# Turning the input of the query product on VectorE instead of TensorE, and moving one softmax scan, in a four-layer graph network kernel

## The chip, the cores and the metric

The kernel runs on one core of a Trainium2 chip. A core has five engines that run side by side and wait for each other through semaphores: TensorE (PE in the profile; its weight loads are listed as PEld), VectorE (DVE), ScalarE (ACT), GpSimd (POOL) and SyncE (SP, which here only issues transfers). Sixteen DMA engines move data between the device memory and the on-chip memory SBUF. TensorE writes its results into PSUM[...]. The metric is the device time of one execution, in microseconds. Before the change it was 3124.89 us, the median of three runs from 3123.66 to 3126.61.

## The reference

The input x has 128 graphs of 128 nodes with 256 features each, in float32. Four layers follow each other, and each is `x = layernorm(x + layer(x))`. The change touches the beginning of layer 0 alone, a graph attention:

```python
Xq = (H @ W_lin.T).reshape(bt, n, h, dh)
Xv = (H @ W_val.T).reshape(bt, n, h, dh)
e = jnp.einsum('behd,hd->beh', jax.nn.leaky_relu(Xq[:, src] + Xq[:, dst], 0.2), a)
e = e + jnp.log(A0[src, dst] + EPS)[None, :, None]
m = jax.ops.segment_max(e.transpose(1, 0, 2), src, num_segments=n)
ex = jnp.exp(e_t - m[src])
attn = ex / jax.ops.segment_sum(ex, src, num_segments=n)[src]
Y = jax.ops.segment_sum(attn[..., None] * Vt, src, num_segments=n)
...
return Y @ W_out.T
```

Here H is x, and there are 512 edges, 4 heads of 64 features. Layer 1 mixes over the graph and multiplies by weights three times (256 to 512 to 1024 to 256 features, ReLU between), layer 2 multiplies by three weight matrices and mixes with parts of the adjacency, and layer 3 is a two-layer network with two batch norms over all nodes, so it needs a pass over all graphs before its second half.

## The kernel before

**Tiling.** The graphs are worked on in 32 quads of four. A quad's x in the layout nodes x (graph, feature) is one tile of 128 partitions and 1024 floats, 512 KB. A product with weights contracts over features, so features have to lie on the partitions: the input must be transposed first.

**Staging.** `start` and `iteration_0` fill the pipeline; then `iteration(k)` runs for k = 1 to 32, and in each pass five quads are in work at different stages: layer 3 of quad a = k-1, layer 1 of c = k, the attention output of b = k+1, the softmax of e = k+2, and the queries and values of g = k+3. Quads 4 to 31 pass through this as g, in 28 passes. All instructions are recorded in the order in which the code writes them (a manual schedule): each engine executes its own in that order, and waits on semaphores where one needs another engine's result. Pools of tiles with a fixed number of buffers hand out SBUF and PSUM; a tile that takes a used buffer waits for its last reader.

**Products in seven parts.** Most products are split into 2x2 blocks and done in seven block products instead of eight (class `Seven`, and by hand in `second`), with sums of blocks ahead (S1 to S4 by `sums_a`, T1 to T4 by `sums_b`, on VectorE) and totals behind.

**The stretch around the change.** `second(c, between)` is the largest product of layer 1: fourteen steps of four matmuls each (L580), with copies on ScalarE (`keep`, L586), totals on VectorE (`total`, L592) and ReLUs on ScalarE (`relu`, L596). After step i it calls `after(i)`, which runs what the caller put into `between[i]`; this is how work of other quads is laid between the block products. In the passes concerned, `between[11]` holds the first step of the softmax of e (a transpose of its scores on TensorE, L385, and four copies by ScalarE, L387), then `values_in(g, quads[g].xg)`, then `query_sums(g)`. `values_in` (L236) transposes the quad's x: eight 128x128 transposes on TensorE (L245) into two PSUM tiles, which VectorE copies to SBUF as `xt` (L247). `query_sums` (L318) then makes S1 to S4 out of blocks of `xt` (L181 to L184, tile `xs`). `between[12]` holds the next two softmax steps, the two scans of the running maximum (L389, L391). Behind step 13 comes the last total of `second`.

**What follows in a pass.** The load of the next quad's x, `load_x(g + 1, "xg", 1, xpool)` (L205), into the only buffer of its tag; the remaining softmax steps (L394 and on); `stage_f` (L801), whose result `ag` ScalarE copies out (L804); then the queries of g (`queries`, L289, with L306 for its kept parts) and `hidden` (L837, with sums L188 to L191) in turns. The queries are written to device memory (`spill`, L268) by a DMA that SyncE issues, and gathered from there by GpSimd along the edges (L336); VectorE works on the gathered rows (`score`, L368 to L371). SyncE issues its transfers in order: the store of x3 (L788), the load of xg, the spill, the store of z (L858), the load of the attention weights (L427), the load of xr.

**Blocks of a product.** `node_blocks(tiles, room)` takes two tiles that hold two graphs each, in which `tiles[j][:, :, c, :]` is half c of the features of graph pair j. It is called by `query_sums` and by `first_seven`.

Of the kernel before, what the change touches and what calls it, by code (L numbers as in the profile page):

```python
# [8 lines left out]
F32 = mybir.dt.float32  # L9
# [17 lines left out]
def gnn_stack(ctx: ExitStack, tc: tile.TileContext, x, adj, w_qv_t, a, w_out_t, src, dst,  # L27
# [14 lines left out]
    nc = tc.nc  # L42
    B, N, D = x.shape
    H, DH = a.shape
    E = src.shape[0]
    P = 128
    assert N == P and D == 2 * P and E == 4 * P and H * DH == D and DH == 64
    NE = E // P
    DC = D // P
    QB = 4  # L50
# [34 lines left out]
    xpool = ctx.enter_context(tc.tile_pool(name="xpool", bufs=1))  # L85
# [43 lines left out]
    with ExitStack() as phase:  # L129
# [63 lines left out]
        quads = [Quad() for _ in range(NQ)]  # L193

        def cload(shape, name, ap, eng=None, dtype=F32, pool=cst):
            t = ctile(shape, name, dtype, pool)
            (eng or nc.sync).dma_start(t, ap)
            return t
# [4 lines left out]
        def load_x(q, tag="xr", bufs=3, pool=wk):  # L203
            t = pool.tile([P, QB, D], F32, tag=tag, name=f"{tag}{q}", bufs=bufs)
            nc.sync.dma_start(t, x[q * QB:(q + 1) * QB].rearrange("b n d -> n b d"))  # L205
            return t

        quads[0].xr = load_x(0)
        wqv = cload([P, DC, 2 * D], "wqv", w_qv_t.rearrange("(c p) f -> p c f", p=P), pool=xpool)
        a_sb = cload([P, N], "adj", adj)  # L210
# [22 lines left out]
        def temp(name):  # L233
            return wk.tile([P, 512], F32, tag="t", name=name, bufs=6)
# [42 lines left out]

        def node_blocks(tiles, room):

            a = {f"A{j + 1}{c + 1}": tiles[j][:, :, c, :] for j in range(2) for c in range(2)}  # L280
            for i in range(4):
                a[f"S{i + 1}"] = room[i // 2][:, (i % 2) * 256:(i % 2 + 1) * 256].rearrange("p (b n) -> p b n", b=2)
            sums_a(a, a)
            return a
# [13 lines left out]
        def queries(k, kept_at):  # L298
# [16 lines left out]

            return Seven(node_product(blocks, queries.blocks), part, out)

        def query_sums(k):  # L318
            quads[k].x_blocks = node_blocks(quads[k].xts, [temp("xs") for _ in range(2)])

        def gather(k):

# [179 lines left out]
        def first_seven(k):  # L502

            s = quads[k]
            room = room_of("adc", 4)
            a = node_blocks([s.mx[0], s.mx[2]], room)

            def part(bank, i):

                to = room[2 + i % 2]  # L510
                nc.scalar.copy(to, bank)
                return to

            def out(row, col, bank, kept_):
                h1 = temp("h1")
                if kept_ is not None:
                    nc.vector.tensor_add(h1, bank, kept_)
                nc.scalar.activation(h1, bank if kept_ is None else h1, AF.Relu)
                for t in range(2):
                    for c in range(2):  # L520
                        s.h1[2 * row + t, 2 * col + c] = h1[:, (2 * t + c) * P:(2 * t + c + 1) * P]

            return Seven(node_product(a, first_seven.blocks), part, out)
# [377 lines left out]
        def iteration(k):  # L901
            a, c, b, e, g = k - 1, k, k + 1, k + 2, k + 3
            has_c, has_b, has_e, has_g = c < NQ, b < NQ, e < NQ, g < NQ
            if has_b and b > 2:
                quads[b].xr = load_x(b)
            if has_c:
                late_sums(c)
            parts = quads[a].layer2
            if not has_c:

                h = quads[a - 1].hidden
                h.p6()
                for _ in range(4):
                    next(parts)
                next(parts)
                h.p7()
                for _ in parts:
                    pass

                def amid():  # L920
                    run(h.p4, h.p3)
                    hidden_stats(a - 1)

                stage_f(a, amid)
                for i in range(K3):
                    hidden_last(a, i)
                return
            steps = softmax_parts(e) if has_e else iter(())
            if has_c:
                between = {i: [] for i in range(14)}  # L930
                for i in (0, 1, 2, 3, 5, 7):
                    between[i].append(lambda: next(parts, None))
                between[11].append(lambda: next(steps, None))
                if has_g:
                    between[11] += [lambda: values_in(g, quads[g].xg), lambda: query_sums(g)]
                between[12] += [lambda: next(steps, None)] * 2
                if has_e:
                    for c_, i in enumerate((0, 2, 4)):
                        between[i].append(lambda c_=c_: score(e, c_ + 1))
                if has_b:  # L940
                    for j, i in enumerate((5, 8, 9, 10)):
                        between[i].append(lambda j=j: by_row(b, j))
                second(c, between)
            if has_g and g + 1 < NQ:
                quads[g + 1].xg = load_x(g + 1, "xg", 1, xpool)
            elif has_g:
                kept["w2t"] = xpool.tile([P, K3, D], F32, tag="xg", name="l3w2", bufs=1)
                nc.sync.dma_start(kept["w2t"], l3_w2_t.rearrange("(c p) f -> p c f", p=P))
            if has_c:
                room = room_of("m2", 7)  # L950
            next(steps, None)
            if has_g:
                q = queries(g, room[:3])
            stage_f(a)
            if not has_b:
                last_sums()
                h = quads[a].hidden = hidden(a, room[5:] + room[3:5])
                for _ in third(c, 0):
                    pass
                rest = third(c, 2)  # L960
                next(rest)
                third_mix(c, 0)
                third_norm(c, 0)
                for _ in rest:
                    pass
                h.p1()
                third_mix(c, 2)
                third_norm(c, 2)
                lower = kept["m2"][:, :3 * 512].rearrange("p (t f) -> p t f", t=2)
                quads[c].layer2 = layer2(c, None, lower)  # L970
                next(quads[c].layer2)
                run(h.p5, h.p2)
                next(quads[c].layer2)
                return
            h = hidden(a, room[5:] + room[2:4])
            if has_g:
                q.p1()
            next(steps, None)
            if has_g:
                run(q.p5, q.p2, q.p6)  # L980
            run(h.p1, h.p5)
            next(steps, None)
            if has_g:
                q.p7()
            run(h.p2, h.p6)
            next(steps, None)
            if has_g:
                run(q.p4, q.p3)
                spill(g)
            h.p7()  # L990
            if has_b:
                aggregate(b)
            run(h.p4, h.p3)
            hidden_stats(a)
            if has_g:
                gather(g)
            if has_b:
                stage_a(b)
            for _ in third(c, 0):
                pass  # L1000
            if has_e:
                attention(e)
                scatter(e)
            rest = third(c, 2)
            mix1(b, 0)
            mix1(b, 2)
            third_mix(c, 0)
            next(rest)
            w = first_seven(b)
            third_norm(c, 0)  # L1010
            next(rest)
            run(w.p1, w.p5, w.p2)
            next(rest)
            if has_g:
                score(g, 0)
                gather_last(g)
            w.p6()
            next(rest, None)
            w.p7()
            third_mix(c, 2)  # L1020
            w.p4()
            w.p3()
            quads[c].layer2 = layer2(c, b)
            next(quads[c].layer2)
            third_norm(c, 2)
            next(quads[c].layer2)
# [56 lines left out]
        def late_loads():  # L1083
            nc.sync.dma_start(w3_sb, w3.rearrange("(c p) f -> p c f", p=P))
            for c in range(DC):
                nc.sync.dma_start(l2w[:, c, :].rearrange("p (k f) -> p k f", k=3),
                                  l2_w[:, c * P:(c + 1) * P, :].rearrange("k p f -> p k f"))
            nc.sync.dma_start(l3w1, l3_w1_t.rearrange("(c p) f -> p c f", p=P))
            quads[4].xg = load_x(4, "xg", 1, xpool)

        def small_loads():
            nc.sync.dma_start(bias, bass.AP(tensor=l2_bias.tensor, offset=l2_bias.offset, ap=[[0, P], [1, D]]))
# [226 lines left out]
    with ExitStack() as phase:  # L1319
        bufs = phase.enter_context(tc.tile_pool(name="bufs", bufs=1))  # L1320
# [36 lines left out]
        with tc.manual_schedule(engines=None):  # L1357
# [157 lines left out]
            for q in range(1, NQ - 1, 2):  # L1515
                if q + 2 < NQ - 1:
                    pairs.append(begin(q + 2))
                d, n = q // 2, len(pairs)
# [128 lines left out]
```

## Time and profile before

| | |
|---|---|
| median of three runs | 3124.89 us |
| profiled run, span on the core | 3121.2 us |
| granted TensorE clock | 0.997 |
| TensorE busy | 3074.9 us, 99% of the span |
| VectorE busy | 2305.4 us, 74% |
| ScalarE busy | 1376.0 us, 44% |
| GpSimd busy | 653.1 us, 21% |
| share of the DMA engines, queue of SyncE | 16.8% |
| transposes of xg on TensorE (L245) | 232, each 273 ns, 30.1 us busy in all |
| copies of them by VectorE (L247) | 56, each 680 ns |
| load of xg | 29, 512 KB each, median 3.8 us from issue to landing |

A line of a group names the source line, the engine, the operation, the tiles as output<-input, the shapes and the count; then the time in which at least one of the group ran, the mean length of one in ns, and the time that the engine was idle just before them, with what ended it. The busy time of TensorE counts overlapping matmuls once. A line of the timeline gives the start in microseconds from the span's start, the length, the engine, and the same names; equal instructions that follow each other are merged, and brackets hold the idle time before. A line of the windows gives a stretch, its length, the busy time of PE, PEld, DVE, ACT and POOL with the numbers of instructions, the granted clock, the share of the DMA engines and GB/s.

### The profile page before, as it was taken

The page shows a single profiled execution, that of the slowest core. Times are in us where ns is not written, and L with a number is a line of the kernel's source. Part 1 is how long each engine was busy: PE and PEld are TensorE (multiplying, and loading weights), DVE is VectorE, ACT ScalarE, POOL GpSimd, SP SyncE. Part 2 cuts the span into 40 slices and gives each one's busy share as a digit, 9 for nine tenths or more (in the row PEclk, how much of TensorE's full clock was granted, in tenths as well). Part 3 has the DMA queues.
Part 4 walks back from the last instruction along what each step waited for, and adds up shares of the span by engine and source line. Part 5 has one row for each costly group of instructions (what it writes and reads, how often), then busy time and mean ns, then how long its engine had stood idle before and what let it go on. Part 6 is the DMA issues. An engine that isn't in the chain of part 4 may idle for free. (4 is left out here: it accounts for less than half of the span.)

```text
span 3121.2 us, 39833 instructions
## 1 busy us (share of the span) xinstructions
PE 3074.9 (99%) x14800; PEld 2404.0 (77%) x14800; DVE 2305.4 (74%) x4599; ACT 1376.0 (44%) x2547; POOL 653.1 (21%) x536
## 2 busy tenths in 40 slices
PE   8999999999999999999999999999999999999998
PEld 4788888888888888888888888888888887874444
DVE  8877777777777777777777777777777776458888
ACT  3344443334444444443344444444433444326668
POOL 3311112222212111122222111211222220001135
PEclk9999999999999999999999999999999999999999
DMA  5633233333333332333333333323333331005457
GB/s 183 160 102 96 78 92 109 102 102 109 109 102 83 108 97 80 91 107 102 102 109 109 102 85 106 100 77 95 102 103 101 109 109 42 21 28 203 175 196 275
DMA packets 117473, 340.05 MB, mean 109 GB/s; under 512 B 14880, under 2 KB 51616, under 8 KB 108960
## 3 DMA queue, kind: packets, MB, share of 16 engines
q0 software_dynamic: 44688, 148.40, 19.3%
q1 hardware_dynamic: 70832, 188.18, 16.8%
q8 instruction: 118, 1.93, 0.3%
q10 hardware_dynamic: 1760, 0.92, 0.1%
q14 instruction: 75, 0.61, 0.1%
HBM read 252.00 MB, written 85.46 MB: 108 GB/s over the span
## 5 line engine op out<-in xcount | busy, mean ns | idle before, releaser
L580 PE MATMUL ph<-m,w 128*128 128x256 f32 x2048 | 473.1, 379 | 0.0
L660 PE MATMUL p<-w,h 128*128 128x256 f32 x2048 | 462.8, 379 | 0.0
L580 PEld LDWEIGHTS ph<-m,w 128*128 128x128 f32 x2048 | 386.8, 190 | 77.9 <-issue 14.8
L660 PEld LDWEIGHTS p<-w,h 128*128 128x128 f32 x2048 | 388.9, 190 | 66.4 <-issue 7.9
L336 POOL DMA_INDIRECT zs<-qd,src_idx x120 | 116.7, 972 | 1356.0 <-DMA qd<-qt 1321.1
L580 PE MATMUL ph<-m,w_s 128*128 128x256 f32 x1536 | 357.7, 379 | 0.4 <-DVE h L592 0.4
L580 PEld LDWEIGHTS ph<-m,w_s 128*128 128x128 f32 x1536 | 291.7, 190 | 53.6 <-issue 14.8
L336 POOL DMA_INDIRECT zs<-qd,dst_idx x120 | 189.1, 1576 | 339.5 <-DMA zs<-qd,src_idx 331.9
L586 ACT COPY u<-ph 128x512 f32<-128x512 f32 x128 | 75.0, 586 | 355.0 <-PE ph L580 355.0
L418 POOL DMA_INDIRECT attd<-at,att_idx x128 | 141.7, 1107 | 343.1 <-DMA attd<-at,att_idx 255.3
L596 ACT ACTIVATE h<-h 128x512 f32<-128x512 f32 x192 | 121.6, 633 | 138.8 <-DVE h L592 138.8
L113 ACT ACTIVATE ln_sd<-ln_mv,eps 128x2 f32<-128x2 f32 x192 | 55.9, 291 | 276.4 <-DVE ln_mv L108 276.4
L370 DVE TENSOR_TENSOR zs<-zs,a_bc 128x1024 f32<-128x1024 f32 x125 | 153.1, 1225 | 4.3
L368 DVE SCALAR_TENSOR_TENSOR zs<-zs 128x1024 f32<-128x1024 f32 x125 | 151.3, 1210 | 6.3 <-DMA zs<-qd,dst_idx 4.3
L371 DVE TENSOR_REDUCE scores<-zs 128x16 f32<-128x1024 f32 x125 | 152.4, 1220 | 4.3
L723 ACT COPY x2k<-y 128x384 f32<-128x384 f32 x192 | 92.0, 479 | 138.5 <-PE y L716 114.2
L106 DVE BATCH_NORM_STATS2 ln_st<-xr 128x6 f32<-128x256 f32 x384 | 144.5, 418 | 6.6
L121 DVE TENSOR_SCALAR xr<-xr,ln_mv,ln_rs 128x256 f32<-128x256 f32 x384 | 143.5, 416 | 7.0
L592 DVE TENSOR_TENSOR h<-ph,u 128x512 f32<-128x512 f32 x128 | 86.9, 679 | 71.9 <-PE ph L580 54.5
L437 ACT COPY adc<-ad 128x512 f32<-128x512 f32 x125 | 133.4, 1070 | 5.9 <-DMA ad<-attd 5.9
L684 POOL TENSOR_TENSOR xb<-xr,bias 128x512 f32<-128x512 f32 x64 | 99.1, 1549 | 150.8 <-DVE xr L121 143.7
L537 PE MATMUL pm<-wt_t,h 128*128 128x128 f32 x1024 | 126.8, 277 | 0.0
(359 smaller groups left out, 6075.9 us busy)
## 6 DMA issues: line engine op xcount, KB each, us to landing
ad<-attd SPq DMA_DIRECT2D x32, 1024.0 KB, 4.8
zd<-z SPq DMA_DIRECT2D x31, 1024.0 KB, 7.2
zl<-zd SPq DMA_DIRECT2D x62, 512.0 KB, 3.6
xr<-in_x_dram SPq DMA_DIRECT2D x32, 512.0 KB, 7.2
x3d<-xr SPq DMA_DIRECT2D x32, 512.0 KB, 2.6
x3l<-x3d SPq DMA_DIRECT2D x32, 512.0 KB, 5.1
out_dram<-x3l POOLq DMA_DIRECT2D x31, 512.0 KB, 5.8
xg<-in_x_dram SPq DMA_DIRECT2D x29, 512.0 KB, 3.8
```

Source lines behind the costliest of these rows:

```text
L106: nc.vector.bn_stats(st[:, i, :], r[:, i, :])
L121: nc.vector.tensor_scalar(r[:, i, :], r[:, i, :], mv[:, i, 0:1], rs[:, i:i + 1], op0=ALU.subtract, op1=ALU.mult)
L336: nc.gpsimd.indirect_dma_start(out=s.z[c], out_offset=None, in_=s.qd, in_offset=bass.IndirectOffsetOnAxis(ap=idx[:, c:c + 1], axis=0), com ...
L368: nc.vector.scalar_tensor_tensor(z, z, SLOPE, z, op0=ALU.mult, op1=ALU.max)
L370: nc.vector.tensor_mul(z3, z3, a_bc.unsqueeze(1).to_broadcast([P, QB, D]))
L371: nc.vector.reduce_sum(s.es[:, c, :], z.rearrange("p (r d) -> p r d", d=DH), axis=AX.X)
L418: nc.gpsimd.indirect_dma_start(out=ad, out_offset=bass.IndirectOffsetOnAxis(ap=att_idx[:, c:c + 1], axis=0), in_=s.at[:, c, :], in_offset= ...
L437: (copy or nc.scalar.copy)(s.adc[:, j * H:(j + 1) * H, :], s.ad.rearrange("p (s r) -> p r s", r=R)[:, j * H:(j + 1) * H, :])
L537: nc.tensor.matmul(pm[:, c // 2, c % 2, :], quads[k].h1[i, c], wt_t, start=True, stop=True)
L580: nc.tensor.matmul(bank[g][:, i].rearrange("p b n -> p (b n)"), wa[:, c, f:f + P], s.m2[:, blk_b, c].rearrange("p b n -> p (b n)"), start= ...
L596: nc.scalar.activation(h, h if src_ is None else src_, AF.Relu)
L660: nc.tensor.matmul(p3[:, t * D:(t + 1) * D], s.h2[f // 2][:, f % 2, j + t, :], w3_sb[:, f, :], start=(f == 0), stop=(f == K2 - 1))
```

## The change

TensorE no longer transposes the input of the query product for quads 4 to 31. Instead the load already places it in blocks, and VectorE finishes the work. VectorE's transpose turns each block of 32 partitions by 32 elements by itself. So `load_turned` reads x in pieces of 32 features (128 bytes) of a node, and puts the 32-feature block i of half c of the features onto partitions 32 i to 32 i + 31: there, for each block of 32 nodes, a 32x32 block lies nodes by features. Turned in place, it gives features on all 128 partitions and nodes along the free dimension. It takes eight transfers (two halves c, four blocks i), each with 32 partitions x 16 pieces x 32 floats, in place of one. `turn(k)` then transposes half c of the tile by one VectorE instruction on 128x512 floats, two in all, straight from SBUF to SBUF.

`turn(g)` is put into `between[9]`, two block products ahead of `query_sums(g)`, which stays in `between[11]`. The two tiles `xt` are now split by feature half and not by graph pair, so `node_blocks` takes its blocks from lists; nothing else in the other caller changes. The second of the two maximum scans moves from step 12 to step 13, so that it stands behind the last total of `second`.

What it is for: to free TensorE of eight transposes in each pass, and to let the last total, and the ReLU behind it, go ahead of a scan that nothing near it waits for.

```diff
+        B = 32
+        def load_turned(q):
+            t = xpool.tile([P, DC, QB * N], F32, tag="xg", name=f"xg{q}", bufs=1)
+            xq = x[q * QB:(q + 1) * QB].rearrange("b (j n) d -> n (b j) d", n=B)
+            for c in range(DC):
+                for i in range(P // B):
+                    d0 = c * P + i * B
+                    nc.sync.dma_start(t[i * B:(i + 1) * B, c, :].rearrange("p (m d) -> p m d", d=B), xq[:, :, d0:d0 + B])
+            return t
...
         def node_blocks(tiles, room):
-            a = {f"A{j + 1}{c + 1}": tiles[j][:, :, c, :] for j in range(2) for c in range(2)}
+            a = {f"A{j + 1}{c + 1}": tiles[j][c] for j in range(2) for c in range(2)}
...
+        def turn(k):
+            s = quads[k]
+            s.xts = [temp("xt") for _ in range(DC)]
+            for c in range(DC):
+                nc.vector.transpose(s.xts[c], s.xg[:, c, :])
+
         def query_sums(k):
-            quads[k].x_blocks = node_blocks(quads[k].xts, [temp("xs") for _ in range(2)])
+            s = quads[k]
+            s.x_blocks = node_blocks([[t[:, j * 256:(j + 1) * 256].rearrange("p (b n) -> p b n", b=2) for t in s.xts]
+                                      for j in range(2)], [temp("xs") for _ in range(2)])
...
-            a = node_blocks([s.mx[0], s.mx[2]], room)
+            a = node_blocks([[s.mx[j][:, :, c, :] for c in range(DC)] for j in (0, 2)], room)
...
                 between[11].append(lambda: next(steps, None))
                 if has_g:
-                    between[11] += [lambda: values_in(g, quads[g].xg), lambda: query_sums(g)]
-                between[12] += [lambda: next(steps, None)] * 2
+                    between[9].append(lambda: turn(g))
+                    between[11].append(lambda: query_sums(g))
+                for i in (12, 13):
+                    between[i].append(lambda: next(steps, None))
...
-                quads[g + 1].xg = load_x(g + 1, "xg", 1, xpool)
+                quads[g + 1].xg = load_turned(g + 1)
...
-            quads[4].xg = load_x(4, "xg", 1, xpool)
+            quads[4].xg = load_turned(4)
```

## The prediction

> **What bounds the kernel now.** I read the page first: its table of engines, then the slices over time, to see whether one engine sets the pace and for how long.
>
> ```profile
> PE 3074.9 (99%) x14800; PEld 2404.0 (77%) x14800; DVE 2305.4 (74%) x4599; ACT 1376.0 (44%) x2547; POOL 653.1 (21%) x536
> ...
> PE   8999999999999999999999999999999999999998
> ...
> PEclk9999999999999999999999999999999999999999
> ```
>
> TensorE is busy in every slice, at an undiminished clock. A busy PE need not be a PE at its peak, so I took the windows of three successive passes of `iteration`, cut where the score transpose L385 starts:
>
> ```profile
> 1309.60:1395.30 85.70, 85.70 (x434) 70.62 (x433) 63.36 (x125) 35.76 (x68) 16.78 (x14) 1.00 0.34 99
> 1395.30:1481.10 85.80, 85.80 (x435) 70.65 (x434) 63.37 (x125) 35.87 (x68) 17.19 (x14) 1.00 0.35 99
> 1481.10:1566.80 85.70, 85.70 (x434) 70.60 (x433) 63.37 (x125) 35.77 (x68) 16.63 (x14) 1.00 0.35 99
> ```
>
> A pass lasts 85.7 us, and the third column, PE, fills it. VectorE (DVE, fifth) fills 63.4 of it, the DMA engines a third. Passes repeat to a hundredth of a microsecond. So a pass is as long as the sum of what PE has to stream, plus short stalls. Work taken from PE shortens a pass by its own length, unless a wait moves in.
>
> The groups by shape then give the work concerned, and the timeline of one pass its surroundings:
>
> ```profile
> L247 DVE COPY xt<-pt 128x512 f32<-128x512 f32 x56 | 35.8, 680 | 0.0
> ...
> L245 PE MATMUL pt<-ident,xg 128*128 128x128 f32 x232 | 30.1, 273 | 0.0
> ```
>
> ```profile
> 1479.19 0.69 DVE L592 TENSOR_TENSOR h<-ph,u 128x512 f32<-128x512 f32 x1 [0.52 <-ACT u L586]
> ...
> 1481.07 0.27 PE L385 MATMUL pe<-ident,scores 128*128 128x128 f32 x1
> 1481.08 0.91 PEld L245 LDWEIGHTS pt<-ident,xg 128*128 128x128 f32 x8
> 1481.18 1.04 PE L245 MATMUL pt<-ident,xg 128*128 128x128 f32 x8
> 1481.27 0.69 DVE L592 TENSOR_TENSOR h<-ph,u 128x512 f32<-128x512 f32 x1 [1.39 <-PE ph L580]
> 1481.88 1.28 DVE L247 COPY xt<-pt 128x512 f32<-128x512 f32 x2
> ...
> 1482.06 1.89 PE L580 MATMUL ph<-m,w 128*128 128x256 f32 x8
> 1482.25 0.38 SPq L205 DMA_DIRECT2D xg<-in_x_dram  x1
> ...
> 1487.05 0.65 DVE L592 TENSOR_TENSOR h<-ph,u 128x512 f32<-128x512 f32 x1
> ...
> 1487.73 0.63 ACT L596 ACTIVATE h<-h 128x512 f32<-128x512 f32 x1 [2.63 <-DVE h L592]
> ...
> 1489.86 0.73 PEld L289 LDWEIGHTS y<-wqv_s,xs 128*128 128x128 f32 x4 [0.21 <-ACT m L306]
> ```
>
> The reader is to see three things. The first of the eight transposes starts at 1481.18 and the product behind them at 1482.06: they hold PE for 0.88 us (110 ns each, though one is 273 ns long: they overlap). VectorE sits idle for 1.39 us ahead of the total at 1481.27. And the last total of `second`, at 1487.05, stands behind two scans, which makes ScalarE late.
>
> **What the Trainium skill says.** "TensorE: Matmul & The Clock Gate", Part 4, gives about 275 ns for a PE transpose in one kernel's context, with the result in PSUM, so that a copy has to follow. The trace agrees on the length (273 ns), but it is the 110 ns from start to start that can be saved. "Vector Engine (DVE) Microarchitecture Reference", section 3.8, says of the transpose mode that it is "Pipelined to sustain one element per cycle per lane", in 32x32 blocks; no row of the kernel before shows one. "DMA: Bandwidth & Descriptors", Specifications, wants at least 512 B for line rate, with a fixed cost per small piece under its bandwidth section. The packet records of this trace agree on the fixed part: 1024 B pieces take 46 ns, 512 B pieces 27 to 32, 32 B pieces 15.
>
> **Part 1, transposes leave PE.** In the built program PE loses 28 groups of eight transposes, for quads 4 to 31, and keeps the rest in the same order (quad 3 keeps its eight, hence 232 in the row and 224 removed). Per pass 0.88 us by the timeline. As a check: 256-column products start every 0.213 us (eight in 1.70), so 128 columns need 0.107, times eight 0.85. Over 28 passes 23.9 to 24.6 us; I take 24.2. Two PSUM banks per pass are asked for no more, so later tiles reuse banks freed earlier, never later.
>
> **Part 2, VectorE transposes instead of copying.** Removed: two copies out of PSUM, 2 x 0.68 us. Added: two transposes of 128x512 f32 from SBUF. The price is unknown here. From below: one element per cycle, the same as the 0.68 us of a plain 128x512 operation between SBUF tiles (L553 in the timeline, 0.68). From above: 1.21 us, what the scans L389 to L400 need for 512 elements. I take 0.69, so 1.38 for both and nothing net on VectorE. They stand behind the total that starts at 1479.19 and ends at 1479.88; so they end at 1481.26, and the next total could not start before 1481.27. The idle 1.39 us hides them. At 1.21 they would end at 1482.30: the total is 1.0 us late, but the sums and scans behind it have room: VectorE idles 1.06 us ahead of L188 at 1489.36, and what L189 writes by 1490.12 is first read by PE at 1491.69. PE pays nothing at either end.
>
> **The added wait on VectorE.** Each transpose waits for four loads. They are issued in the pass before, some 75 us earlier. Queued behind it are the total (the ReLU and a PSUM bank wait for that) and the sums S1 to S4, which end at about 1483.5; PE reads them at 1488.16 in the old pass, 1487.28 in the new one.
>
> **Part 3, the load in 128-byte runs.** One DMA of 512 runs of 1 KB becomes eight, each of 512 runs of 128 B: 4096 runs a quad, 256 per DMA engine. By the packet records a run is between the 15 ns of 32 B and the 32 ns of 512 B; I take 17. So 4.4 us, against 32 x 46 ns = 1.5 us now; 8.2 us at the upper end. Issuing costs SyncE 8 x 0.38 = 3.1 us, beside it. The issue can start when VectorE has read the tile, at about 1481.3, since the DMA is no longer behind PE; the last of the eight also waits for the semaphore of the x3d store, issued at 1478.70 with 2.7 us to landing, so 1481.4. Behind them on SyncE stands the spill of the queries (L268), which issues at 1496.82 now and some 0.9 us earlier then. So there are 14.6 us for a load of 6 to 11 us, latency included, and the packet records have nothing else on the DMA engines from 1485.7 to 1497.6. Even a late spill has room: the first gathered chunk, its second gather issued at 1504.87 with 7.6 us to landing, is there at 1512.5, and VectorE reads it at 1522.06: 9.6 us. I cost part 3 at nothing.
>
> **Part 4, one scan behind the last total.** VectorE's work is the same; only the order changes. The last product now ends at 1485.3 + 0.2 - 0.9 = 1484.6, the first scan near 1484.8, so the total runs from 1484.8 instead of 1487.05, and its ReLU on ScalarE near 1485.5 instead of 1487.73. ScalarE's copies of ag (1488.27, right behind that ReLU although PE had finished near 1487.4) then follow PE, and so does L306, whose lateness holds PE at 1489.86: there four products take 1.11 us instead of 1.03, 0.08 us a pass. If that goes, 28 x 0.08 = 2.3 us; I count half to two thirds of it, 1.3. The softmax is not delayed, since its subtraction comes at about 1487 in place of 1487.63.
>
> **Sum.** 24.2 + 1.3 = 25.5 us off 3124.9: 3099.4. The start of the kernel also loads quad 4 in 128-byte runs, behind the late weights at 94 us; the load of ad behind it waits for its scatter until 113.41 anyway, so nothing.
>
> **Rivals.**
> First, VectorE takes over as the bound of this stretch. For it: the transposes are put into the only gap there, and 63.4 of 85.7 us are taken. Were a transpose to run at a quarter rate, 2.3 us each, VectorE would work without a break from 1479.88: 4.6 for the pair, 0.69 total, 1.56 sums, 1.23 and 1.21 scans, 0.65 total, 0.67 subtraction, 0.84 for L188 and L189, so to 1491.33, where PE wants it at 1490.73. PE loses 0.6 of 0.96 us; 28 x 0.36 = 10: 3115. Against it: the section above, and no element-wise row here is near that rate.
>
> Second, the small runs choke the DMA queue, and the spill and the gathers behind it come late. For it: the skill's "VectorE: DVE Perf Modes", The three transpose paths, warns that a plain copy which transposes by strides is 19 times slower than the crossbar; 19 x the 3.8 us of the load now would be 72 us. Up to 14.6 + 9.6 = 24 us cost nothing; 30 us would cost 6 - 0.9 = 5 us a pass, 28 x 5 = 140: 3265, slower than before. Against it: the runs here stay 128 B long on both sides, and the 32 B pieces in the trace took 15 ns.
>
> Third, a wait replaces the transposes: PE arrives 0.88 us sooner at a product that waits for ScalarE or VectorE (in the view of waits PE's weight loads are held by ScalarE at L289 most, 18.7 us in 32 times) and gives most of it back: 3120, no change. Against it: those producers start from PE's own products and move with it.
>
> **How the numbers follow.** Forecast 0.85, VectorE bound 0.07, DMA 0.05, wait 0.03. The time is the forecast's. Below, 24.6 + 2.3 and a microsecond or two of spread give 3096. Above, the range takes in a lost part 4, and about half of the VectorE case, to 3108; what is left out is under 0.15. Faster by over 0.2% (6.2 us) are the forecast and the first rival, 0.92; within it the third, 0.03; slower the second, 0.05.
>
> **What would show it.** Right: passes of 84.8 us, no PE rows for quads 4 to 31 at L245, transposes of about 0.69 us ending before the next total, the eight loads landed before the spill is issued, and the first of L289's y products on wqv_s at 1.03. Wrong: a DVE transpose over 2 us, a spill whose landing is late with gathers that VectorE waits for, or a pass still near 85.7 with new idle time of PE's loads behind DVE or ACT.

## The result and the profile after

The changed kernel took 3103.60 us, the median of four runs from 3099.01 to 3104.86, beside 3124.81 us for the kernel before: a ratio of 0.9929, 95% interval 0.9912 to 0.9946. The forecast was 3099.4, with a range of 3096 to 3108. Measured again the ratio was 0.9916, 0.9902 to 0.9929.

The page after, its engines and the queue of SyncE's transfers (packets, MB, share of 16 engines; the queue had 70,832 packets and 16.8% before):

```profile
PE 3047.4 (98%) x14576; PEld 2382.0 (77%) x14576; DVE 2311.5 (75%) x4599; ACT 1388.0 (45%) x2547; POOL 652.6 (21%) x536
...
q1 hardware_dynamic: 174320, 188.19, 18.5%
```

TensorE has 224 instructions and 27.5 us of work less. VectorE has as many instructions as before and 6 us more of busy time. The queue has two and a half times the packets for the same bytes, and is little busier. The windows of three successive passes, cut at the score transpose as before:

```profile
1297.40:1382.20 84.80, 84.80 (x426) 69.83 (x425) 63.52 (x126) 36.24 (x67) 16.74 (x14) 1.00 0.37 100
1382.20:1467.00 84.80, 84.80 (x426) 69.83 (x425) 63.50 (x126) 36.28 (x68) 17.28 (x14) 1.00 0.37 100
1467.00:1551.80 84.80, 84.80 (x427) 69.84 (x426) 63.76 (x126) 36.26 (x68) 16.91 (x14) 1.00 0.37 100
```

PE still fills a pass, which is now 84.8 us. To a hundredth, the commonest distance of two score transposes went from 85.73 to 84.78: 0.95 us, over 28 passes 26.7. The group by shape of the new instruction:

```profile
L336 DVE STREAM_TRANSPOSE xt<-xg 128x512 f32<-128x512 f32 x56 | 36.2, 685 | 0.0
```

And the timeline of one pass around it (line numbers are 22 higher than before, and 13 higher at L218, L281, L302 and L319):

```profile
1465.12 0.69 DVE L614 TENSOR_TENSOR h<-ph,u 128x512 f32<-128x512 f32 x1 [0.51 <-ACT u L608]
...
1465.73 1.29 DVE L336 STREAM_TRANSPOSE xt<-xg 128x512 f32<-128x512 f32 x2
...
1467.01 0.27 PE L407 MATMUL pe<-ident,scores 128*128 128x128 f32 x1
...
1467.05 4.05 SPq L218 DMA_DIRECT2D xg<-in_x_dram  x8
1467.12 1.89 PE L602 MATMUL ph<-m,w 128*128 128x256 f32 x8
1467.21 0.69 DVE L614 TENSOR_TENSOR h<-ph,u 128x512 f32<-128x512 f32 x1 [0.18 <-PE ph L602]
...
1470.77 0.69 DVE L614 TENSOR_TENSOR h<-ph,u 128x512 f32<-128x512 f32 x1
...
1471.50 0.63 ACT L618 ACTIVATE h<-h 128x512 f32<-128x512 f32 x1 [0.82 <-DVE h L614]
...
1474.95 1.03 PE L302 MATMUL y<-wqv_s,xs 128*128 128x256 f32 x4
...
1481.80 0.34 SPq L281 DMA_DIRECT2D qd<-qt  x1
```

The product of `second` starts 0.11 us behind the score transpose, where it came 0.99 us behind it. The two VectorE transposes lie where VectorE was idle for 1.39 us: they end at 1467.02, and VectorE still waits 0.18 us for its next total. That total is not late (0.20 us behind the score transpose in both kernels). The eight loads are issued by 1471.10, and the spill behind them not before 1481.80. The last total starts 3.76 us after the score transpose instead of 5.98, ScalarE's ReLU behind it waited 0.82 us instead of 2.63, and the first products on `wqv_s` take 1.03 us where they took 1.11 in the kernel before:

```profile
1489.89 1.11 PE L289 MATMUL y<-wqv_s,xs 128*128 128x256 f32 x4
```

### The profile page after: what moved, and what is told of

The parts are those of the page before. It is cut to its first block, busy times and chain, and to the rows that moved or that the text cites. A ratio compares the mean times of both kernels' runs of the same rounds, so it can differ in the third digit from the quotient of the medians.

```text
span 3097.3 us, 39721 instructions
## 1 busy us (share of the span) xinstructions
PE 3047.4 (98%) x14576; PEld 2382.0 (77%) x14576; DVE 2311.5 (75%) x4599; ACT 1388.0 (45%) x2547; POOL 652.6 (21%) x536
## 5 line engine op out<-in xcount | busy, mean ns | idle before, releaser
L745 ACT COPY x2k<-y 128x384 f32<-128x384 f32 x192 | 92.0, 479 | 139.5 <-PE y L738 114.2
L559 PEld LDWEIGHTS pm<-wt_t,h 128*128 128x128 f32 x1024 | 121.2, 192 | 1.4 <-issue 1.3
```

The lines of the kernel that those rows point to most:

```text
L559: nc.tensor.matmul(pm[:, c // 2, c % 2, :], quads[k].h1[i, c], wt_t, start=True, stop=True)
```

## Experiments

All ratios are to the kernel before, on the same chip, with the 95% interval. A pass is the commonest distance of two score transposes in the profile. In the two profiles of the changed kernel it agrees to 0.01 us, and so tells far smaller things apart than the whole time does.

**1. The changed kernel again**, no edit.

> The changed kernel once more, to see how much of the give-back belongs to it. Its passes are 0.955 us shorter in the trace, 28 of them 26.7 us, but the median fell by 21.2 us. If the end stage (the store of the output, after the last batch norm) only spreads from run to run, as it does for the kernel before: 3098 to 3101, a saving of 24 to 27 us. If the change itself lengthens the end stage: again 3103 to 3105, a saving of 20 to 22 us.

3101.32 against 3127.37 us, 0.9916 (0.9902 to 0.9929); pass 84.78. The saving was 26 us, that of the first measurement 21.

**2. The scan alone.** The kernel before, with only the second maximum scan moved behind the last total.

```diff
-                between[12] += [lambda: next(steps, None)] * 2
+                for i in (12, 13):
+                    between[i].append(lambda: next(steps, None))
```

> The kernel before with only the second maximum scan moved behind the last total. Theory (PE streams, and the late copy of a kept part held it for 0.08 us a pass): passes of 85.65 us, 2.3 us saved, 3122.5, and the first product of L289 on wqv_s back from 1.11 to 1.03 us. Rival (the scan's place costs PE nothing, the 0.08 us went with the transposes): no change, 85.73 us a pass.

0.9991 (0.9984 to 0.9997), pass 85.66: 0.08 us a pass, 2.2 us over 28 passes; the medians differ by 3.1. The stall at the first products on `wqv_s` is gone.

**3. The turning alone.** The changed kernel with both scans at step 12 (experiment 2's edit, backwards).

> The changed kernel with both scans left in step 12, so only the turning moves. Theory: passes of 84.86 us (0.88 less than before), 24.6 us saved, with the 0.08 us stall at L289 still there. Rival (the turning ahead of the total also brings the total and the copies forward, so that the scan's place no longer matters): passes of 84.78 as with both parts.

3101.05 us, 0.9916 (0.9902 to 0.9929), pass 84.78. The stall at `wqv_s` is gone here too, without the scan's move, as the rival had it and not my theory of 84.86. So that move adds nothing to the turning at step 9.

**4. One load of 1 KB runs.** The changed kernel with the old load; VectorE turns what lies in the tile.

```diff
-                nc.vector.transpose(s.xts[c], s.xg[:, c, :])
+                nc.vector.transpose(s.xts[c], s.xg.rearrange("p b d -> p (b d)")[:, c * 512:(c + 1) * 512])
...
-                quads[g + 1].xg = load_turned(g + 1)
+                quads[g + 1].xg = load_x(g + 1, "xg", 1, xpool)
...
-            quads[4].xg = load_turned(4)
+            quads[4].xg = load_x(4, "xg", 1, xpool)
```

> The changed kernel with the old single load of x in runs of 1 KB in place of the eight loads in runs of 128 B; VectorE turns the same sizes, but blocks that lie in the wrong places, so layer 0 gets wrong queries and values. Theory (the load is hidden): the same 84.78 us a pass and the same time as the changed kernel. Rival (the small runs cost DMA time that the rest of the kernel pays): 2 to 5 us faster than the changed kernel, near 3098.

3102.02 us, 0.9917 (0.9904 to 0.9931), pass 84.785. The load in small runs costs nothing that shows (the changed kernel on the same chip took 3101.32).

**5. The small-run load alone.** The kernel before with the new load; TensorE transposes what lies in the tile.

```diff
-                    between[11] += [lambda: values_in(g, quads[g].xg), lambda: query_sums(g)]
+                    between[11] += [lambda: values_in(g, quads[g].xg.rearrange("p c (b d) -> p (c b) d", b=2)), lambda: query_sums(g)]
...
-                quads[g + 1].xg = load_x(g + 1, "xg", 1, xpool)
+                quads[g + 1].xg = load_turned(g + 1)
...
-            quads[4].xg = load_x(4, "xg", 1, xpool)
+            quads[4].xg = load_turned(4)
```

> The kernel before with only its load of xg replaced by the eight loads in 128-byte runs; TensorE transposes as before, but blocks that lie in the wrong places, so layer 0 gets wrong queries and values. Theory (the load is hidden): 85.73 us a pass and the time of the kernel before within 1 us. Rival (small runs are paid for in DMA time): 2 to 5 us slower.

1.0004 (0.9995 to 1.0012), pass 85.74, like the kernel before.

**6. The load four and eight times over**, to find where its room ends.

```diff
-            for c in range(DC):
+            for c in [c for _ in range(8) for c in range(DC)]:
```

(and the same with 4.)

> The changed kernel with the turned load done four times over, 32 transfers, some 17 us of issuing and moving. Eight times made the spill 21.9 us late and cost 13.6 us a pass, so the spill may be about 8 us late. Theory (a threshold): the spill 3 to 4 us late and passes of 84.78 us, no change against the changed kernel. Rival (a late spill costs PE from the start, about 0.6 us for each): passes of 86.5 to 87 us.

> The changed kernel with the turned load done eight times over, 64 transfers of 64 KB into the same tile: some 31 us of issuing and moving. Theory (a load has 14 us until the spill of the queries behind it on SyncE is due, and the gathers have some 9.6 us more; beyond that VectorE waits for gathered rows and PE for VectorE): the spill 17 us late, passes of 88 to 93 us, 3190 to 3330. Rival (GpSimd waits 47 us a pass for the spill anyway, so there is far more room): 84.78 us a pass, no change.

Four times: 3107.07 us, 0.993 (0.9914 to 0.9947), pass 84.783. SyncE's own timeline, start and length:

```profile
1474.88 17.32 SPq L218 DMA_DIRECT2D xg<-in_x_dram  x32
1492.45 0.34 SPq L281 DMA_DIRECT2D qd<-qt  x1
```

Here the spill (`qd`) is issued 17.57 us after the first load, 17.9 in the median pass, where it is 14.75 us in the changed kernel. Being 3 us late costs no pass anything. What this kernel is slower by lies ahead of the passes: the first one starts at 202.8 us, in the other kernels, the one with eight loads apart, at 194.5 to 197.7.

Eight times: 3498.93 us, 1.1191 (1.1166 to 1.1216), passes of 98.5 in the median. SyncE's timeline, then the view of VectorE's waits (us in total, times, longest):

```profile
1508.69 36.45 SPq L218 DMA_DIRECT2D xg<-in_x_dram  x64
1545.38 0.34 SPq L281 DMA_DIRECT2D qd<-qt  x1
```

```profile
DVE zs L390 <- DMA zs<-qd,dst_idx: 356.3, 28, 15.5
```

This is the path of the prediction's second rival, though what makes the spill late is here the issuing and not a slow queue: the spill waits behind 64 issues, the gathers behind the spill, and VectorE waits for the gathered rows 28 times, once ahead of the passes and in each of the 27 passes with a load. What TensorE loses shows in the timeline of one pass and in its windows:

```profile
1171.43 2.08 PE L302 MATMUL z<-w,adc 128*128 128x256 f32 x4 [10.76 <-DVE h L539]
```

```profile
1163.00:1176.66 13.66, 5.23 (x20) 4.76 (x21) 7.54 (x14) 2.42 (x5) 5.13 (x5) 0.50 0.63 108
1176.66:1220.00 43.34, 43.34 (x201) 34.54 (x200) 38.02 (x65) 19.18 (x38) 6.31 (x6) 1.00 0.33 88
```

In the median pass the spill comes 36.1 us after the first load instead of 14.75, 21.3 us later, and this product starts 11.3 us late. So the slack was about 10 us; the prediction had 9.6. A pass lost more than that, 13.7 us: during TensorE's wait its granted clock falls to 0.5, and stays there for 10 to 14 us in each of these passes (17 in one), so that the first products after the wait run slowly (2.08 us for four, 1.03 in the changed kernel), and another 2.2 us go. I had expected passes of 88 to 93. I took 0.48 us for an issue, where one took 0.57, and had nothing for the clock.

**7. The transposes twice and three times over**, to find VectorE's room.

```diff
-                nc.vector.transpose(s.xts[c], s.xg[:, c, :])
+                for _ in range(3):
+                    nc.vector.transpose(s.xts[c], s.xg[:, c, :])
```

(and the same with 2.)

> The changed kernel with every transpose on VectorE done twice: 1.3 us more of VectorE's time. Three times cost 1.07 us a pass for 2.6 us of work, so the room should be about 1.5 us. Theory (a threshold): 84.78 to 84.85 us a pass. Rival (every added microsecond of VectorE costs PE 0.4): 85.3 us a pass.

> The changed kernel with every transpose on VectorE done three times: 2.6 us more of VectorE's time ahead of the total. Theory (VectorE's room in this stretch is about 1.5 to 2 us; behind that, the total, its ReLU and the copy of the first kept part hold PE at L289): passes of 85.3 to 85.9 us, half or more of the gain gone, 3115 to 3130. Rival (VectorE is busy for 63 of 85 us, so it has room for 2.6 us more): 84.78 us a pass.

Twice: 3099.61 us, 0.9907 (0.989 to 0.9923), pass 84.782. Three times: 1.001 (1.0001 to 1.0018), pass 85.85. So 1.4 us more of VectorE in this stretch are free and of 2.7 us more 1.07 are paid. The payer is TensorE at its first product on `wqv_s`, in all 28 passes, behind ScalarE's kept copy `m` of the first `y` product.

**8. The turning without its place.** The transposes at step 11, where TensorE's stood; the scan still moved.

```diff
-                    between[9].append(lambda: turn(g))
-                    between[11].append(lambda: query_sums(g))
+                    between[11] += [lambda: turn(g), lambda: query_sums(g)]
```

> The changed kernel with the turning moved from step 9 to step 11, directly ahead of the sums, where the copies stood before. Theory (VectorE's idle time ahead of the total hid it; 1.3 us later, the last total, its ReLU and ScalarE's copies of ag and of the kept part are late again, as in the kernel before): 84.86 to 85.0 us a pass, 2 to 6 us slower than the changed kernel, with a stall back at L289 on wqv_s. Rival (the place is free as long as the turning is done before the sums): 84.78 us a pass.

3103.02 us, 0.9921 (0.9905 to 0.9938), pass 84.785. My theory, that the transposes had to lie in the idle time at step 9, falls: the sums and the first scan come later, and nobody waits.

**9. The turning without its place and without the scan's move**: edit 8, and both scans back at step 12. This leaves the work of VectorE in the order of the kernel before, and takes only TensorE's transposes away.

> The changed kernel with the turning at step 11 and both scans at step 12: the order of the kernel before, only with VectorE turning in place of TensorE. Theory (the 0.08 us stall of PE at L289 on wqv_s goes when the last total comes earlier, whichever part brings it forward, and stays when neither does): 84.86 us a pass, the stall back. Rival (the stall went with the transposes themselves): 84.78 us a pass.

3129.07 against 3126.98 us, 1.0006 (0.9997 to 1.0015), pass 85.75. No gain is left at all. Neither theory had said so. The timeline of one of its passes (score transpose at 1484.15):

```profile
1489.00 1.21 DVE L413 TENSOR_TENSOR_SCAN m<-reset_b,m 16x512 f32<-16x512 bf16 x1
...
1490.14 0.65 DVE L614 TENSOR_TENSOR h<-ph,u 128x512 f32<-128x512 f32 x1
...
1490.83 0.63 ACT L618 ACTIVATE h<-h 128x512 f32<-128x512 f32 x1 [3.03 <-DVE h L614]
...
1491.36 1.05 ACT L826 COPY ag<-pa 128x512 f32<-128x512 f32 x2
...
1492.30 0.60 ACT L319 COPY m<-y 128x512 f32<-128x512 f32 x1
...
1492.96 1.13 PE L302 MATMUL y<-wqv_s,xs 128*128 128x256 f32 x4 [0.70 <-ACT m L319]
```

and the view of TensorE's waits of the same kernel, its first line (none of the kind appears in the changed kernel):

```profile
PE y L302 <- ACT m L319: 19.7, 28, 0.7
```

The last total stands behind two scans, ScalarE's ReLU waits 3.03 us for it, the copies of `ag` and the kept copy of the first `y` product stand behind that ReLU, and TensorE, which arrives 0.88 us sooner than before, waits at the first product on `wqv_s`. (A matmul's wait is counted from the modelled end of the one before; from start to start TensorE loses 0.87 us at this place, and the first product then takes 0.10 us longer, which makes the 0.97 us between this pass and the changed kernel's.)

**10. VectorE's operation with one input, in the last stage.** Not about the change itself but about where 2 to 3 us of the gain went (see below).

```diff
-                nc.vector.scalar_tensor_tensor(nm, mvs[q][:, :, 0], -1.0, rs, op0=ALU.mult, op1=ALU.mult)
+                for i in range(QB):
+                    nc.vector.tensor_scalar(nm[:, i:i + 1], mvs[q][:, i, 0:1], rs[:, i:i + 1], -1.0, op0=ALU.mult, op1=ALU.mult)
```

> The changed kernel, but in the last stage the coefficients nm = -mean x rs (L1589, one VectorE operation on 128x4 with two SBUF tiles as inputs) are computed by four operations on one column each, with rs as a per-partition factor: one SBUF tile as input. The question is where the 2 to 3 us go that the last stage is longer in the kernels with short passes (113.3 to 116.4 us from its first transposes of agg, against 111.0 to 111.7 in most others). Theory: VectorE's operation with two SBUF inputs is held until a GpSimd addition beside it ends (1.3 to 1.9 us instead of 0.16, 2 times in the last stage of the kernel before, 4 times in that of the changed kernel), ScalarE starts its next activations 1.5 us late, and TensorE waits 1.6 us for agg. Then no nm operation here takes over 0.4 us, and TensorE's waits of 1.6 us for agg are gone (the two of 4.4 and 1.1 us at the start of the stage stay). The last stage gets shorter by up to 1.6 us for each, 107 to 109 us, less what three more small operations a quad cost: 0.1 us each by the 0.15 us of the reciprocal beside them, up to 10 us over 32 quads if VectorE (88% busy there) sets the pace. Passes stay at 84.78. Rival: the long operations are not held by GpSimd, or do not matter; then waits of 1.6 us for agg stay, 2 or more, and the stage is 113 us or more.

3100.36 us, 0.9918 (0.9904 to 0.9931), pass 84.785. No `nm` operation takes over 0.22 us, though 43 of the 128 overlapped an addition of GpSimd by 0.09 us or more, and TensorE's waits of 1.6 us for `agg` are gone. The stage still takes 113.0 us: the four operations of a quad overlap, but take 0.58 us together in place of 0.16, where I had allowed for 0.3 more, and TensorE now has small waits there instead. So it is shown that this operation is not held when it has one SBUF tile as input, but not what the holding costs the stage, and no time is won.

## Why the prediction was right, and where it was not

**The bound, and the length of a pass.** Right. It said passes of 84.8 by a bound of TensorE's streaming, and they are 84.78.

**The sum.** 25.5 us were forecast. The commonest pass gives 28 x 0.95 = 26.7. In the profiled pair the 28 passes together save 25.99 us (2401.04 to 2375.05), the start and the stretch behind the passes 0.75, and the last stage loses 2.81 (111.65 to 114.46), which makes the 23.93 us between the two spans. The repetition measured 26 us. That the sum fits is in part luck: its two terms are not worth what it says when each is taken by itself, and it holds because this change happens to contain both.

**Part 1, transposes leave TensorE: 0.88 us.** The size is right (experiment 9 finds just this as a wait of 0.87), but not the claim that it could be had alone. With VectorE's work in its old order it is worth nothing: 85.75.

**Part 4, the scan: 0.08 us a pass, counted as a separate 1.3 us.** This is the step that failed. Its size alone is right (0.08 us in experiment 2), but the terms do not add. On top of the turning at step 9 the scan adds nothing (84.784 without it, 84.781 with it); with the turning at step 11 it is worth the whole 0.97 us (85.75 without, 84.785 with). Places in one pass of each kernel, medians over 20 passes, in us after the score transpose; "TensorE free" is 0.21 us after the start of the product before, which is when the next one starts without a wait:

| kernel | last total starts | kept copy ends | TensorE free | product on wqv_s starts | pass |
|---|---|---|---|---|---|
| before | 5.97 | 8.74 | 8.81 | 8.81, first one 0.08 longer | 85.73 |
| scan alone | 4.73 | 7.87 | 8.81 | 8.81 | 85.66 |
| changed | 3.77 | 7.00 | 7.94 | 7.94 | 84.78 |
| turning alone | 4.94 | 7.70 | 7.94 | 7.94 | 84.78 |
| transposes twice | 4.59 | 7.36 | 7.94 | 7.94 | 84.78 |
| turning at 11, scan moved | 4.74 | 7.51 | 7.94 | 7.94 | 84.785 |
| turning at 11, scans as before | 5.99 | 8.75 | 7.94 | 8.81, first one 0.10 longer | 85.75 |
| transposes three times | 6.09 | 8.85 | 7.94 | 8.90, first one 0.10 longer | 85.85 |

Two paths meet at this product: TensorE's own, and VectorE's total, transposes or copies, sums, scans, last total, then ScalarE's ReLU, two copies and the kept copy. In the kernel before both were equally long, to 0.08 us: the stall that I read as a trifle of 2.3 us was the tip of a second bound right below the first. Taking 0.88 us from TensorE's path leaves the other one standing. Either half of the re-ordering shortens that one, by 0.9 to 1.2 us, and either is enough. The pair of moves thus buys one thing twice: the copy ends 0.94 us ahead of TensorE, where one move leaves 0.24 or 0.43. Not all of that is room. In the three kernels of the table with a stall the product is through its wait some 0.15 us after the copy ends (8.75 to 8.81 and 0.10 more, for instance), so about 0.8 us are to spare with both moves, 0.1 with the turning alone and 0.3 with the scan moved and the turning at 11. I formed this reading after the runs; it fits all eight rows, and no run was made to test it ahead.

**The third rival, a wait that replaces the transposes.** I gave it 0.03 because "those producers start from PE's own products and move with it". That sentence is wrong. The chain starts from a product of `second` that stands ahead of the removed transposes, so it does not move when they go. Experiment 9 is this rival, in full and at the line I had named. It did not come true because the change also re-orders VectorE, not for the reason that I gave.

**Part 2, VectorE.** Right: 0.69 us forecast, 0.685 measured, hidden in the idle time ahead of the total. My bound of 1.21 us as harmless holds too: it adds 1.05 us a pair, and experiment 7 adds 1.4 for nothing. The first rival (2.3 us each, a loss of 0.6 a pass) would add 3.2; 2.7 more cost 1.07. So its mechanism exists, at a price no transpose here came near, and by this estimate its loss would have been larger than I said. The place is another one, too: I looked for room at the sums L188 and L189, but what gives way first is the kept copy.

**Part 3, the load.** Right, with nothing on the path. 4.4 us were forecast for a quad; the packets of one took 4.5 from the first to the last (13 ns each, below the 15 to 32 that I took for bounds, but they wait for the issues). Issuing took 4.05 instead of 3.1 us, since one of a row of eight takes 0.51 us and not the 0.38 of a single one. It is issuing by SyncE, and not the engines' time for small runs, that chokes first: in experiment 6, with 64 issues, a packet still takes 13 ns, and the last one ends 1.5 us after the last issue, where it is 1.4 us in the changed kernel. The second rival's 72 us came from a factor of 19 that is said of a copy with a large innermost stride at its destination, beside the crossbar; put on a plain load with runs of 128 B it was no fit: from the first issue to the last landing the eight loads took 5.9 us.

**The last stage**, of which the prediction says nothing. It lasts from the first transposes of `agg` to the end, and its length goes with how often VectorE's `nm` operation (L1589 after) took over 0.4 us there: 111.0 to 111.7 us with two such (before, scan alone, small-run load alone, transposes three times), 113.3 to 114.2 with three (the repetition, turning alone, one load, eight loads), 114.0 to 116.4 with four or five (changed, experiments 8 and 9, four loads, transposes twice). The timeline of the changed kernel at the first one:

```profile
3012.31 1.92 DVE L1589 SCALAR_TENSOR_TENSOR nm<-mv,rs 128x4 f32<-128x4 f32 x1
...
3012.92 1.28 POOL L1566 TENSOR_TENSOR x3l<-x3l,shift_bc 128x512 f32<-128x512 f32 x1
...
3014.26 1.09 ACT L1601 ACTIVATE x3l<-x3l,nm,rs 128x256 f32<-128x256 f32 x2 [1.51 <-DVE nm L1589]
...
3016.99 0.93 PE L1561 MATMUL pt<-ident,agg 128*128 128x128 f32 x4 [1.62 <-ACT agg L1374]
```

An operation on 4 elements a partition that otherwise takes 0.16 us ends 0.03 us after GpSimd's addition beside it. ScalarE waits 1.51 us for it, and TensorE 1.62 us a step later. The Trainium skill, "SBUF — State Buffer", Who interferes with whom, says that a VectorE instruction with two SBUF inputs contends with a GpSimd instruction that reads SBUF, and calls that "an exclusive lock". The trace agrees that it is held to the end of the other, 0.03 us after it in all four. The first of the four starts 0.61 us ahead of the addition, during GpSimd's issue of a store; other `nm` operations that start during such an issue take 0.16 us, and GpSimd's times are rough in the profile, so what held this one until the addition began stays open. With one SBUF tile as input (experiment 10) none is held. Nor is it settled how the holding lengthens the stage. TensorE's granted clock also falls to 0.5 for 3.4 us, once for 6.8, behind some of its waits in the middle of the stage: twice or three times where four or five operations were held, once at most where two or three were. That the kernels with short passes had more of these meetings may be chance or follow from their later timing: experiment 9 has long passes and four of them. This stays open.

## What to carry to other kernels

A stall of hundredths that comes back in every pass, at a place where two engines meet, need not be a small gain to be added to the sum. In this kernel it said that a second path was as long as the first, so that what was taken from one had to be taken from both. Before pricing work removed from the bounding engine, follow the nearest wait behind it back to its start, and ask whether that start lies behind the removed work or ahead of it. Here taking away 0.88 us of TensorE's work brought nothing, moving the scan alone brought 0.08, and both together 0.95.

## What the runs showed of the hardware

- VectorE's 32x32 transpose of 128x512 f32 took 685 ns, as a plain operation of that shape does (680 to 690).
- 4096 pieces of 128 B took 13 ns each in the packet records, less than the 15 ns of 32 B pieces in the kernel before (on GpSimd's queue). From the first issue to the last landing a 512 KB load took 5.9 us in them, in eight issues, against 3.8 in one issue of 1 KB pieces.
- SyncE's issues in a row took longer each: 0.38 us for one, and for the first of a row; 0.51 on average in a row of eight, 0.54 in one of 32, 0.57 in one of 64.
- TensorE's granted clock fell to 0.5 while it waited some 11 us in each pass of the kernel with eight loads, and stayed there for 10.24 or 13.65 us in all but one of these passes.
- A VectorE operation that sums blocks of 128x128 f32, 0.28 us alone, took 2.68 us beside GpSimd's addition. It happened in two passes of the repetition, and they are the two that are 0.94 and 0.95 us longer than the commonest. This is the first of them:

```profile
927.84 2.68 DVE L183 TENSOR_TENSOR x2s<-x2t 128x128 f32<-128x128 f32 x1
...
928.49 1.87 POOL L706 TENSOR_TENSOR xb<-xr,bias 128x512 f32<-128x512 f32 x1
...
933.14 0.91 PE L738 MATMUL y<-l2w_s,x2t 128*128 128x384 f32 x2 [0.68 <-ACT x2k L745]
```
